# Node chunks of every fourth node, and the loads of a graph-network kernel rearranged over the queues

## The chip, the cores and the metric

The kernel runs on one core of a Trainium2 chip. The metric is the device time of one execution, in microseconds (us). A core has five engines with their own instruction streams: TensorE (PE in the profile) for matmuls, VectorE (DVE), ScalarE (ACT), GpSimd (Pool) and SyncE (SP), which issues DMAs. ACT and Pool issue DMAs too. Engines wait for each other by semaphores; DMA engines, 16 of them, move the data that the queues hand them.

## The reference

Four layers work on x (8 batches, 2048 nodes, 64 channels) with one adjacency matrix adj (2048 × 2048), whose rows hold one value or zero. `_layernorm` is over the channels. Layer 0 has weights of its own for each node:

```python
# layer 0
h = maximum(_layernorm(x), 0)
w = einsum('nd,dkio->nkio', embedding, weight)      # D = 16, K = 3
A_stack = [I, adj, 2 * adj @ adj - I]
x_g = einsum('knm,bmc->bnkc', A_stack, h)
x = x + einsum('bnki,nkio->bno', x_g, w) + embedding @ bias
# layer 1: node 0 set to intervention_value, then three times
effects = einsum('nm,bmd->bnd', adj, v)
v = relu([v, effects] @ W1.T + b1) @ W2.T + b2      # x = x + v
# layer 2: x = x + ((adj @ h) scaled twice, summed, + b_nl) @ w_out.T + b_out
# layer 3: attention, whose mask adj > 0.5 leaves the mean over nodes: x = x + elu(mean(h))
```

## The kernel before

The 8 batches go in four pairs p; a tile of activations holds 128 nodes by (4 node chunks j) by (2 batches × 64 channels), 256 KB, and a pair has four such blocks nb of 512 nodes. Node n of a block is partition n mod 128 of chunk n div 128, so one partition's data of a chunk and batch is a run of 64 floats, 256 B, in x and in the output. The signs of adj stay in SBUF for the whole kernel as `BT` (16 rows m of 128 nodes by 2048), and each product with adj is scaled afterwards by one value per column (`crow`). A product operand is split in a high and a low part (H and L, `halves` L201), so each matmul is done twice. `scaled` (L213, its operation at L214) takes a product out of PSUM times `crow`. DRAM scratch `hs` and `xs` keep the normalised and the running activations; `crowD`, `biasD`, `t1D` and `MD` keep intermediate results.

**The head** (L390 to L468) is what most of the change touches. Rows of adj are loaded (`load_adj` L304) and turned into signs by ACT, two halves each (`signs` L315). The x blocks of pairs 0 and 1 are loaded (`load_x01` L272, `fill_x` at L126), each by two DMAs of 128 KB: one block on ACT's queue, one on SP's, six on Pool's, between the adjacency rows. They are normalised in eight `tick`s (L395), block (0,0), (1,0), (0,1), (1,1) and so on. A norm (`norm_stages` L153) is: mean (L158, L159) and subtraction (L160) on DVE into a tile z, of which there are three buffers (L155); square on ACT (L164); variance on DVE (L167, L168); power −1/2 on Pool (L170); scale on DVE (L173). Then the block is stored to `hs` from SP (L252 to L256), copied to H on ACT (L206) and subtracted to L on DVE (L208). As soon as a row m has its signs and its block is ready, PE does `step` (L415, matmul L418): eight matmuls for pair 0 into four PSUM banks, and, one row later, six for pair 1 into three. These are 224 matmuls of 128 × 128 by 128 × 512.

The order of work is written by hand: `tc.issue_after` puts an instruction behind a named one, `pool_loads` (L307) chains Pool's DMAs behind a given power, and `plan` (L435) says which rows go behind which power. The diagonal blocks of adj (`load_dg`) give the `cols` (`make_cols`), and these the `crow`s (`make_crow`). `bias_loads` (L334) brings the embedding and the bias, `bias_products` (L347 to L361) makes the bias of each node, with the transpose `pe` at L348. The weights `wt` come by six DMAs on SP (L460 to L468), twice the same data for the two halves of the partitions.

**After the head**, the fourth quarter of pair 1's product (L494) is made, t1 is turned back to node order (L499 and before), and for each p and nb there are a second product (L222) and the stage of the node weights (`node_weights` L616): for each of 32 tiles y of a pair, twelve matmuls listed at L632 and eight DVE operations (L641) that add y times one embedding value into `acc` and `odd` by turns. The block is then normalised for the next layer, stored by Pool (`keep` L607 to L613), and a row of `BT` is stored to `MD` (L708). While that runs, SP loads x again (`load_x`), `biasD`, `crow` and others in the order in which the program names them. `layer1` (L763) has three products per pair, `layer2` (L875) one, `finish2` (L835) adds layer 2 and normalises, `outputs` (L859) adds the elu of the mean (L870) and stores (L873), two DMAs per block. For the last pair the queues of these are Pool, SP, ACT and SP for nb 0 to 3.

Of the kernel before, what the change touches and what calls it, by code (L numbers as in the profile page):

```python
# [14 lines left out]
ALU = mybir.AluOpType  # L15
AX = mybir.AxisListType

EPS = 1e-5
# [24 lines left out]
def uniform_path(  # L43
# [65 lines left out]
    make_identity(nc, ident)  # L109
# [3 lines left out]
    order = [nc.gpsimd.memset(mhalf, -0.5)]  # L113

    def part(nb):
        return slice(4 * nb, 4 * nb + 4)

# [5 lines left out]
    def fill_x(acc, layer, p, nb, queue=nc.sync):  # L123
        if layer == 0:
            for bb in range(2):
                ld = queue.dma_start(  # L126
                    acc[:, :, bb * C:(bb + 1) * C],
                    x[2 * p + bb].rearrange("(j p) c -> p j c", p=P)[:, part(nb), :],
                )
            return ld  # L130
        else:
            nc.sync.dma_start(acc, xs[p][:, part(nb), :])
# [13 lines left out]

    pending = []
    powers, firsts, squares, lows, stored = [], [], [], [], []  # L150
    ahead = []

    def norm_stages(xt, name, done, out_):  # L153

        z = block("z", f"z_{name}", 3)  # L155
        g = groups(z)
        mean = small.tile([P, 8], F32, name="mean")
        nc.vector.tensor_reduce(mean, groups(xt), axis=AX.X, op=ALU.add)  # L158
        nc.vector.tensor_scalar(mean, mean, 1.0 / C, None, op0=ALU.mult)  # L159
        firsts.append(nc.vector.tensor_tensor(  # L160
            g, groups(xt), mean[:, :, None].to_broadcast([P, 8, C]), op=ALU.subtract
        ))
        sq = block("sq", f"sq_{name}", 1)
        squares.append(nc.scalar.activation(sq, z, AF.Square))  # L164
        yield
        var = small.tile([P, 8], F32, name="var", bufs=3)
        nc.vector.tensor_reduce(var, groups(sq), axis=AX.X, op=ALU.add)  # L167
        nc.vector.tensor_scalar(var, var, 1.0 / C, EPS, op0=ALU.mult, op1=ALU.add)  # L168
        rstd = small.tile([P, 8], F32, name="rstd", bufs=3)
        powers.append(nc.gpsimd.tensor_tensor(rstd, var, mhalf, op=ALU.pow))  # L170
        yield
        h = z if out_ is None else out_
        nc.vector.scalar_tensor_tensor(  # L173
            groups(h), g, 0.0, rstd[:, :, None].to_broadcast([P, 8, C]), op0=ALU.max, op1=ALU.mult
        )
        done(h)
        yield
# [35 lines left out]
    def scaled(ps, out, crow):  # L213
        ahead.append(nc.vector.tensor_tensor(out, ps, crow, op=ALU.mult))  # L214
        return out
# [36 lines left out]
    def norm_0(p, nb, also=None, xt=None):  # L252

        def done(z):
            stored.append(
                (nc.gpsimd if xt is None else nc.sync).dma_start(hs[p][:, part(nb), :], z)  # L256
            )
            if also is not None:
                also(z)

        norm_relu(load_x(0, p, nb) if xt is None else xt, f"0_{p}_{nb}", done)
# [10 lines left out]
    def load_x01(queue=nc.sync):  # L272
        p, nb = norm_order[len(x01)]
        nm = f"x_{p}_{nb}"
        if p == 1:
            t = term(1, nm).rearrange("p (j f) -> p j f", j=4)
        else:
            t = block("acc" if nb < 2 else "crow", nm, 2)
        loads.append(fill_x(t, 0, p, nb, queue))
        x01.append(t)  # L280
# [23 lines left out]
    def load_adj(m):  # L304
        loads.append(nc.gpsimd.dma_start(BT[:, m, :], adj[m * P:(m + 1) * P, :]))
# [28 lines left out]
    def bias_loads():  # L334
        bd = spare("H", "bd")
        nc.gpsimd.memset(bd, 0.0)
        with tc.issue_after(stored[-1].ins):
            nc.sync.dma_start(emb, embedding.rearrange("(j p) d -> p j d", p=P))
        for j in range(8):
            ld = nc.sync.dma_start(bd[j * D:(j + 1) * D, j * C:(j + 1) * C], bias)  # L340
        bias_tiles.extend((bd, ld))
# [49 lines left out]
    ticks = [0]  # L391
    rests = []
    ticks_at = (0, 1, 2, 3, 4, 6, 8, 10)

    def tick():  # L395
        go_on()
        while rests:
            rests.pop()()
        last = (lows or firsts or [None])[-1]
        k = ticks[0]  # L400
        if k < len(norm_order):
            p, nb = norm_order[k]
            with tc.issue_after(last.ins) if last else nullcontext():
                norm_0(
                    p, nb,
                    lambda z: hls[p].append(
                        halves(z, f"0_{p}_{nb}", prox if p else None, rests)
                    ),
                    x01[k],
                )  # L410
        if lows:
            ahead.append(lows[-1])
        ticks[0] += 1
# [11 lines left out]
    load_x01(nc.scalar)  # L425
    load_x01()

    def lx(_):
        load_x01(nc.gpsimd)

    row, dia = load_adj, load_dg
    pool_loads(order[0], ((row, 0), (lx, 2), (row, 1), (lx, 3), (row, 2)))
    tick()
    tick()
    plan = {  # L435
        0: (0, ((lx, 4),)), 1: (1, ((row, 3), (lx, 5), (row, 4))),
        2: (2, ((lx, 6), (row, 5), (lx, 7))), 3: (3, ((row, 6), (row, 7), (dia, 0), (dia, 1))),
        4: (4, ((row, 8), (row, 9))), 6: (5, ((row, 10), (row, 11), (dia, 2), (dia, 3))),
        8: (6, ((row, 12), (row, 13))), 10: (7, ((row, 14), (row, 15))),
    }  # L440
    for m in range(NCH):
        if m == 12:
            bias_loads()
        if m in ticks_at:
            tick()
        if m in plan:
            pool_loads(powers[plan[m][0]], plan[m][1])
        if m in (11, 13):
            with tc.issue_after(lows[-1].ins):
                for q in (0, 1) if m == 11 else (2, 3):  # L450
                    make_cols(q)

        signs(m, squares[m] if m in (0, 2, 3) else copies[(0, 0, 1, 0, 2, 3, 4, 4, 5, 6, 7)[min(m, 10)]])
        last = step(0, m, banks[0])
        if m > 0:
            with tc.issue_after(last.ins):
                last = step(1, m - 1, banks[1])
        if m in (13, 14):
            with tc.issue_after(last.ins):
                for nb in (0, 1) if m == 13 else (2, 3):  # L460
                    make_crow(nb)
# [3 lines left out]
    for k in range(K):  # L465
        for hf in range(2):
            with tc.issue_after(bias_tiles[1].ins):
                wt_load = nc.sync.dma_start(  # L468
                    wt[hf * C:(hf + 1) * C, k, :].rearrange("i (d o) -> i d o", d=D),
                    weight[:, k].rearrange("d i o -> i d o"),  # L470
                )
    all_done()
# [135 lines left out]
    def keep(p, nb, acc, name, more=None):  # L608

        norm_relu(acc, name, lambda z: nc.gpsimd.dma_start(hs[p][:, part(nb), :], z))  # L610
        if more is not None:
            nc.gpsimd.tensor_tensor(acc, acc, more, op=ALU.add)  # L612
        kept.append(nc.gpsimd.dma_start(xs[p][:, part(nb), :], acc))  # L613
# [3 lines left out]
    def node_weights(p, nb, terms, between=None):  # L617
# [5 lines left out]
        av = acc.rearrange("p j (b c) -> p j b c", b=2)  # L623
        ov = odd.rearrange("p j (b c) -> p j b c", b=2)
# [32 lines left out]
    for p in range(NP):  # L657
# [27 lines left out]
        for nb in range(NB):  # L685
# [20 lines left out]
            with tc.issue_after(kept[-1].ins):  # L706
                m = 4 * p + nb
                nc.gpsimd.dma_start(MD[m * P:(m + 1) * P, :], BTf[:, m, :])  # L708
# [16 lines left out]
    def rows4(r):  # L725
        return r[:, None, :].to_broadcast([P, 4, 2 * C])
# [45 lines left out]
    def layer1(n, p):  # L772
        hl, gT = ops[n]
        steps = 3
        for s in range(steps):
# [3 lines left out]
            def finish(nb):  # L779
                nm = f"1_{p}_{s}_{nb}"  # L780
                if last:
                    acc = load_x(1, p, nb)
                    nc.gpsimd.tensor_tensor(acc, acc, rows4(b2r), op=ALU.add)
                    pn = back_to_nodes(g_new[nb], w2T, nm)
                    nc.vector.tensor_tensor(acc, pn, acc, op=ALU.add)
                    keep(p, nb, acc, f"2_{p}_{nb}", rows4(rbo))
                else:
                    pn = back_to_nodes(g_new[nb], w1e2, nm)
                    nc.vector.tensor_tensor(pn, pn, rows4(r1e), op=ALU.add)
                    hl_new.append(halves(pn, nm))  # L790
# [46 lines left out]
    def finish2(g):  # L837
# [7 lines left out]
        nc.vector.tensor_tensor(acc, pn, acc, op=ALU.add)  # L845
# [14 lines left out]
    def outputs(p):  # L860
# [7 lines left out]
        for nb in range(NB):  # L868
            acc = accs[NB * p + nb]
            (nc.gpsimd if nb == 0 else nc.vector).tensor_tensor(acc, acc, rows4(y), op=ALU.add)  # L870
            queue = (nc.gpsimd, nc.sync, nc.scalar, nc.sync)[nb] if p == NP - 1 else nc.sync
            for bb in range(2):
                queue.dma_start(  # L873
                    out[2 * p + bb].rearrange("(j p) c -> p j c", p=P)[:, part(nb), :],
                    acc[:, :, bb * C:(bb + 1) * C],  # L875
                )
# [635 lines left out]
```

## The time and the profile before

| What | us |
|---|---|
| median of 3 runs | 1280.17 |
| lowest and highest | 1278.7, 1280.47 |
| profiled execution | 1280.51 |
| its span in the profile | 1278.6 |
| outside the span | 1.9 |

| Engine | busy us | share |
|---|---|---|
| PE matmul | 1217.3 | 95% |
| PE weight load | 862.7 | 67% |
| DVE | 751.4 | 59% |
| Pool | 236.8 | 19% |
| ACT | 182.3 | 14% |

A span runs from the first to the last recorded instruction of the core. Busy is the time in which an engine had at least one operation under way; weight loads lie beside matmuls. The granted clock is the share of full speed that PE was allowed. In the DMA views q0 is Pool's queue[...], q1 SP's and q10 ACT's[...]. The time to landing is from the issue of a DMA to the completion that its semaphore tells.

### The profile page before, as it was taken

Reading aid. Unit: us, or ns where it says so; the run is one execution under the profiler, and the core shown is the slowest. Engines: PE = TensorE matmul, PEld = TensorE weight load, DVE = VectorE, ACT = ScalarE, POOL = GpSimd, SP = SyncE. Lnnn points to the kernel's source line nnn. Section 1 sums busy time; section 2 is a strip of 40 time slices with the busy share of each in tenths; the row PEclk is TensorE's granted clock in tenths of the full one; section 3 lists DMA queues with packets and bytes.
Section 4 is the critical chain, followed back from the end, with each engine's and each line's share of the span. In section 5 each row is a group of like instructions: output and inputs, shape, how many; then the busy total and the mean of one; then the engine's idle time right before and its main releaser. Section 6 shows DMA issues by size and latency. Waiting matters only on the chain.

```text
span 1278.6 us, 15515 instructions
## 1 busy us (share of the span) xinstructions
PE 1217.3 (95%) x5702; PEld 862.7 (67%) x5702; DVE 751.4 (59%) x1936; ACT 182.3 (14%) x281; POOL 236.8 (19%) x244
## 2 busy tenths in 40 slices
PE   4899999999999999999999999999999999999993
PEld 3665554555575556755567888787788787788882
DVE  5445887767746776377654446445543554575653
ACT  5530010000010000000011121112111111211100
POOL 6410211111121111011110024004102400432222
PEclk9999999999999999999999999999999999999996
DMA  8982343323332222122255425433643543524321
GB/s 265 343 208 74 96 112 87 90 70 84 95 105 71 71 79 66 65 62 62 67 141 136 102 93 158 112 92 121 150 117 87 159 116 86 161 95 115 108 58 36
DMA packets 140057, 141.14 MB, mean 110 GB/s; under 512 B 95093, under 2 KB 97141, under 8 KB 137925
## 3 DMA queue, kind: packets, MB, share of 16 engines
q1 hardware_dynamic: 121092, 82.05, 25.2%
q0 software_dynamic: 12160, 49.10, 12.8%
q10 hardware_dynamic: 6720, 8.92, 2.5%
q8 instruction: 47, 0.77, 0.2%
q14 instruction: 38, 0.30, 0.1%
HBM read 95.92 MB, written 35.73 MB: 103 GB/s over the span
## 4 chain that ended last, share of the span: by engine, by line
PE 83%; DMA 6%; DVE 4%; issue 3%; POOL 2%; ACT 1%; SPq 0%; ACTq 0%; POOLq 0%; DVEq 0%
PE bv L222 34%; PE y L632 23%; PE bn L587 4%; PE ph L804 3%; PE bv_0b L222 2%; PE bv_2b L222 2%; DMA BT<-in_adj_dram 2%; PE bv_3b L222 2%; PE bv_1b L222 2%; DMA hb<-hs 1%; POOL rstd L170 1%; PE bv_0a L222 1%; PE bv_3a L222 1%; PE bv_2a L222 1%; PE bv_1a L222 1%
## 5 line engine op out<-in xcount | busy, mean ns | idle before, releaser
L222 PE MATMUL bv<-BT,H 128*128 128x512 f32 x1024 | 426.7, 417 | 0.0
L222 PE MATMUL bv<-BT,L 128*128 128x512 f32 x1024 | 401.2, 392 | 0.0
L222 PEld LDWEIGHTS bv<-BT,H 128*128 128x128 f32 x1024 | 192.6, 188 | 47.9 <-issue 11.6
L222 PEld LDWEIGHTS bv<-BT,L 128*128 128x128 f32 x1024 | 192.9, 188 | 47.3 <-issue 11.5
L641 DVE SCALAR_TENSOR_TENSOR acc<-y,emb,acc 128x128 f32<-128x128 f32 x512 | 176.2, 344 | 65.8 <-PE y L632 62.4
L632 PE MATMUL y<-wt,t0T 64*128 64x512 f32 x512 | 144.2, 608 | 10.0 <-DVE odd L641 10.0
L641 DVE SCALAR_TENSOR_TENSOR odd<-y,emb,odd 128x128 f32<-128x128 f32 x448 | 153.3, 342 | 0.0
L170 POOL TENSOR_TENSOR rstd<-var,mhalf 128x8 f32<-128x8 f32 x64 | 107.9, 1688 | 194.5 <-DVE var L168 184.3
L214 DVE TENSOR_TENSOR g<-bv,crow 128x512 f32<-128x512 f32 x48 | 33.2, 691 | 183.7 <-PE bv L222 183.7
L164 ACT ACTIVATE sq<-z 128x512 f32<-128x512 f32 x64 | 40.4, 631 | 406.5 <-DVE z L160 397.4
L632 PEld LDWEIGHTS y<-wt,t0T 64*128 64x128 f32 x512 | 46.7, 187 | 73.9 <-issue 68.0
L612 POOL TENSOR_TENSOR acc<-acc,wl 128x512 f32<-128x512 f32 x16 | 20.6, 1289 | 297.3 <-DVE z L160 297.2
L613 POOL DMA_DIRECT2D xs<-acc x32 | 18.0, 562 | 276.2 <-DVE acc L649 254.2
L632 PE MATMUL y<-wt,t1T 64*128 64x512 f32 x256 | 67.9, 596 | 0.0
L173 DVE SCALAR_TENSOR_TENSOR z<-z,rstd 128x512 f32<-128x512 f32 x64 | 45.9, 723 | 28.2 <-POOL rstd L170 28.2
L587 PEld LDWEIGHTS bn<-wl,g 128*128 128x128 f32 x384 | 49.5, 191 | 6.3 <-ACT H L206 1.6
L167 DVE TENSOR_REDUCE var<-sq 128x8 f32<-128x512 f32 x64 | 43.5, 679 | 15.8 <-ACT sq L164 15.8
L587 PE MATMUL bn<-wl,g 128*128 128x128 f32 x384 | 51.1, 276 | 1.0 <-DVE var L168 0.5
L749 DVE SCALAR_TENSOR_TENSOR junk<-mt,cols,st 128x512 uint8<-128x512 bf16 x64 | 50.8, 794 | 0.6
L632 PEld LDWEIGHTS y<-wt,t1T 64*128 64x128 f32 x256 | 27.7, 188 | 27.3 <-issue 27.3
L809 ACT ACTIVATE g<-g,b1s 128x512 f32<-128x512 f32 x32 | 23.2, 724 | 139.4 <-DVE g L808 139.3
L160 DVE TENSOR_TENSOR z<-acc,mean 128x512 f32<-128x512 f32 x56 | 38.3, 690 | 6.6 <-DMA hs<-z 5.2
(209 smaller groups left out, 1677.3 us busy)
## 6 DMA issues: line engine op xcount, KB each, us to landing
BT<-in_adj_dram POOLq DMA_DIRECT2D x16, 1024.0 KB, 9.2
crow<-crowD SPq DMA_DIRECT2D x64, 256.0 KB, 3.2
st<-in_adj_dram SPq DMA_DIRECT2D x64, 256.0 KB, 3.4
hs<-z POOLq DMA_DIRECT2D x40, 256.0 KB, 2.8
xs<-acc POOLq DMA_DIRECT2D x32, 256.0 KB, 2.5
MD<-BT POOLq DMA_DIRECT2D x16, 512.0 KB, 5.0
acc<-xs SPq DMA_DIRECT2D x32, 256.0 KB, 3.2
hb<-hs SPq DMA_DIRECT2D x28, 256.0 KB, 3.6
```

The costliest lines, as they stand in the source:

```text
L160: firsts.append(nc.vector.tensor_tensor(g, groups(xt), mean[:, :, None].to_broadcast([P, 8, C]), op=ALU.subtract))
L164: squares.append(nc.scalar.activation(sq, z, AF.Square))
L167: nc.vector.tensor_reduce(var, groups(sq), axis=AX.X, op=ALU.add)
L170: powers.append(nc.gpsimd.tensor_tensor(rstd, var, mhalf, op=ALU.pow))
L173: nc.vector.scalar_tensor_tensor(groups(h), g, 0.0, rstd[:, :, None].to_broadcast([P, 8, C]), op0=ALU.max, op1=ALU.mult)
L214: ahead.append(nc.vector.tensor_tensor(out, ps, crow, op=ALU.mult))
L222: nc.tensor.matmul(ps, hl[m // 4][i][:, m % 4, :], BT[:, m, nb * 512:(nb + 1) * 512], start=(m == 0 and i == 0), stop=(m == NCH - 1 and i ...
L587: nc.tensor.matmul(ps[:, t, :], fT[:, t * P:(t + 1) * P], wmat, start=True, stop=True)
L632: nc.tensor.matmul(y[:, bb, :], terms[k][hs_, ts], wt[hs_, k, dg * 512:(dg + 1) * 512], start=(k == 0), stop=(k == K - 1),)
L641: last = nc.vector.scalar_tensor_tensor(xj, yd, ec, old, op0=ALU.mult, op1=ALU.add)
L749: nc.vector.scalar_tensor_tensor(junk, mt, cols[:, i, :], st, op0=ALU.mult, op1=ALU.not_equal, accum_out=bad[:, i, q:q + 1],)
L804: fill[12] = lambda: nc.tensor.matmul(ph, w1v2 if s else w1vT, gT[nb], start=True, stop=True)
```

## The change

Node n of a block is now partition n div 4, chunk n mod 4: four consecutive nodes lie in one partition. So x, the embedding and the output move in runs of four nodes (1 KB for x and the output, 256 B for the embedding), and a row m of `BT` and `MD` holds every fourth node of a block. Inside a tile that is read from x the order is batch, chunk, channel; helpers give the view that an operation needs (`nodes`, `split`, `each`). `scaled` writes its columns permuted, so that what follows finds the chunks together.

The loads of x go on SP, all eight at its start, one DMA for each block; Pool loads adj alone, seven rows at once, then rows behind the powers of a new plan. The ident tile is made without its helper, its two operations ahead of the loads. The ticks are replaced by `norm_block`, which puts a whole norm on DVE in one order, every second row. Three weight loads are followed by three copies within SBUF. The last pair's stores are one DMA per block, blocks 1, 2, 0, 3 in order, blocks 0 and 2 from ACT, 1 and 3 from SP.

```diff
+    def rows_of(a, m):
+        return a.rearrange("(b p t) n -> b t p n", p=P, t=4)[m // 4, m % 4]
+    def runs_of(a, p, nb):
+        return a[2 * p:2 * p + 2].rearrange("e (b p t) c -> b p e (t c)", p=P, t=4)[nb]
+    def runs(acc):
+        return acc.rearrange("p j f -> p (j f)").rearrange("p (e r) -> p e r", e=2)
+    def nodes(acc):
+        return acc.rearrange("p j f -> p (j f)").rearrange("p (e j c) -> p j e c", e=2, c=C)
...
         if layer == 0:
-            for bb in range(2):
-                ld = queue.dma_start(
-                    acc[:, :, bb * C:(bb + 1) * C],
-                    x[2 * p + bb].rearrange("(j p) c -> p j c", p=P)[:, part(nb), :],
-                )
+            return queue.dma_start(runs(acc), runs_of(x, p, nb))
...
     def scaled(ps, out, crow):
-        ahead.append(nc.vector.tensor_tensor(out, ps, crow, op=ALU.mult))
+        ps, crow = (a.rearrange("p (q t) -> p q t", t=4) for a in (ps, crow))
+        to = out.rearrange("p (t q) -> p q t", t=4)
+        ahead.append(nc.vector.tensor_tensor(to, ps, crow, op=ALU.mult))
...
+    def norm_block(k):
+        stage(k, 0)
+        low()
+        stage(k, 1)
+        stage(k, 2)
...
-    load_x01(nc.scalar)
-    load_x01()
-    pool_loads(order[0], ((row, 0), (lx, 2), (row, 1), (lx, 3), (row, 2)))
-    tick()
-    tick()
+    for _ in norm_order:
+        load_x01(nc.sync)
+    pool_loads(order[0], tuple((row, m) for m in range(7)))
+    for i in range(3):
+        stage(0, i)
+        if i == 2:
+            low()
+        stage(1, i)
     plan = {
...
+        1: (1, ((row, 7), (row, 8))), 2: (2, ((row, 9), (row, 10))),
+        3: (3, ((row, 11), (dia, 0), (dia, 1))), 4: (4, ((row, 12),)),
+        5: (5, ((row, 13), (dia, 2), (dia, 3))), 6: (6, ((row, 14), (row, 15))),
     }
...
     for k in range(K):
-        for hf in range(2):
...
+            wt_load = nc.sync.dma_start(
+                wt[:C, k, :].rearrange("i (d o) -> i d o", d=D),
+                weight[:, k].rearrange("d i o -> i d o"),
+            )
+    with tc.issue_after(wt_load.ins):
+        for k in range(K):
+            nc.sync.dma_start(wt[C:, k, :], wt[:C, k, :])
...
         odd = l0q.tile([P, 4, 2 * C], F32, name="odd")
-        av = acc.rearrange("p j (b c) -> p j b c", b=2)
-        ov = odd.rearrange("p j (b c) -> p j b c", b=2)
+        av, ov = nodes(acc), nodes(odd)
...
-        for nb in range(NB):
+        for nb in (1, 2, 0, 3):
...
-            (nc.gpsimd if nb == 0 else nc.vector).tensor_tensor(acc, acc, rows4(y), op=ALU.add)
-            queue = (nc.gpsimd, nc.sync, nc.scalar, nc.sync)[nb] if p == NP - 1 else nc.sync
-            for bb in range(2):
-                queue.dma_start(
-                    out[2 * p + bb].rearrange("(j p) c -> p j c", p=P)[:, part(nb), :],
-                    acc[:, :, bb * C:(bb + 1) * C],
-                )
+            (nc.gpsimd if nb == 0 else nc.vector).tensor_tensor(
+                nodes(acc), nodes(acc), rows4(y), op=ALU.add
+            )
+            queue = nc.scalar if nb % 2 == 0 and p == NP - 1 else nc.sync
+            queue.dma_start(runs_of(out, p, nb), runs(acc))
```

The signs of each row stand behind a named norm operation on ACT: rows 2 and 3 behind the square of the third block, rows 4 and 5 behind that of the fourth, and so on; the `crow`s are made two rows later, at rows 14 and 15. The embedding is loaded by the same grouping in one DMA of 256 B runs, still behind the last norm's store to `hs`.

## The prediction

> **What bounds the kernel now.** I read the table of windows first, then the waits of TensorE (PE), then the chain of what ended last. Over the span PE is busy 95%, so only its gaps can be shortened, and the windows show most of them at the start. The columns are the busy time and count of each engine, the granted clock, the DMA share and GB/s.
>
> ```profile
> 0.00:20.00 20.00, 4.88 (x12) 3.83 (x13) 10.36 (x23) 9.68 (x12) 12.49 (x22) 1.00 0.87 263
> 20.00:40.00 20.00, 16.45 (x62) 11.95 (x61) 11.01 (x23) 9.87 (x13) 15.07 (x16) 0.92 0.95 289
> 40.00:60.00 20.00, 18.41 (x75) 13.57 (x74) 9.70 (x30) 13.74 (x17) 8.71 (x11) 0.99 0.94 337
> 60.00:80.00 20.00, 19.05 (x90) 14.69 (x89) 6.39 (x23) 8.91 (x9) 1.97 (x4) 1.00 1.11 280
> ```
>
> PE's busy time hides how little is done; its counts tell. The chain steps back-to-back matmuls by 0.23 us, so 20 us hold about 88: the first two windows hold 12 and 62. Meanwhile the DMA engines are 87 to 95% busy. PE's waits, in us in all, times and longest:
>
> ```profile
> PE bv_0a L418 <- ACT H L206: 15.1, 1, 15.1
> PE y L632 <- DVE odd L641: 10.0, 7, 2.9
> ...
> PE bv_0a L418 <- ACT BT L319: 4.5, 4, 1.9
> ```
>
> The first is the start: nothing to multiply until 15.1 us. The second lies in the y stage. The last of the head's chain, and the stall behind the second (start, duration):
>
> ```profile
> 33.48 10.97 DMA BT<-in_adj_dram
> ...
> 54.14 9.42 DMA BT<-in_adj_dram
> 63.58 2.01 ACT BT L319 x2
> ```
> ```profile
> 411.13 4.61 DMA crow_3b<-crowD
> ```
>
> So the head is bound by the arrival of adjacency rows (L305), which come when Pool issues them, and from 65.6 us by PE. Its steps end with the transpose `pe` at 81.5.
>
> [...]While adjacency rows (8 KB packets, q0) stream beside embedding packets of 64 B on SP's queue (q1), the DMA view of 64 to 68 us has one for one; in 70 to 71 us, when q0 runs dry, q1 leaps:
>
> ```profile
> q0 software_dynamic: 225, 1.61, 102.6%
> q1 hardware_dynamic: 226, 0.01, 32.5%
> ```
> ```profile
> q1 hardware_dynamic: 1189, 0.08, 92.2%
> q0 software_dynamic: 32, 0.13, 34.9%
> ```
>
> A small packet thus costs its queue the whole of an 8 KB packet in between. [...]No row of before writes fp32 with a 512 B stride.
>
> **The head, step by step.** Removed from Pool: six x blocks, 12 issues, in pairs of about 1.5 us (9 us); adj rows 0 to 6 are then issued back to back at 0.57 us. Added on SP: eight x DMAs of 256 KB at its start. The first normalised block also needs no Pool issue between its two powers and its data: I put PE's first matmul at 10.5 instead of 15.1.
>
> But SP's queue also carries the stores hs<-z (L256). In before it has one x block ahead of them; in after all eight. DVE's fourth subtract, z of block (1,1), reuses the first of three z buffers (L155), and waits until that buffer's hs store has landed. Behind it on DVE stand L of block (0,1) and every later norm; behind its square on ACT stand the signs of row 4; so PE can do rows 0 to 3 (32 matmuls of pair 0, 18 of pair 1: 50), to about 24 us, and then waits. When does the store land?
> - x has 8 × 256 = 2048 packets of 1 KB. Adj data starts at 4.2 us in before; here the ident operations (0.20 and 0.30 us on Pool's timeline) move ahead of the first issue: 4.5. From about 2.4 to 4.5 at 284 GB/s (a window of before) some 600 to 640 pass; 1408 are left, 88 for each of 16 engines.
> - One for one they go with 88 adj packets per engine, rows 0 to 10, all issued by then. A pair took 4 us × 16 / 225 = 0.284 us with 64 B; 1 KB at 20 GB/s per engine (16 share about 330) adds 0.05: 0.33. So x ends at 4.5 + 88 × 0.33 = 33.5. Where the other packet is dearer (0.38), 37.9.
> - The store follows. Such stores landed in 7.9 us (median) beside adj, 2.5 at the best: I take 4, so 37.5 to 38; both ends 36 and 46.
>
> From 38: subtract 0.69, square 0.63, half a sign 1.04, so row 4 at 40.4. Left are 224 − 50 = 174 matmuls × 0.2276 (20 us / 88) = 39.6, four groups of pt_c 1.9, and 2 for the clock: at 15.1 to 19.6 in before matmuls start 0.43 apart. That is 83.9 against 81.5, **+2.4**. ACT, DVE and Pool need about 5.7 us for each block of two rows after the stall (L170 alone 1.7 to 2.0), PE 28 × 0.2276 = 6.4, so PE bounds. Rows 11 to 15 are issued behind later powers, the last at about 58, landing in some 6; PE wants row 15 after 78. Pool's waits of rows 8 to 15 for a DMA semaphore of an older row can delay the powers queued behind, but those rows landed long before. Moved later, crow and t1T steps (two t1T evictions of 0.69 us ahead of crow copies): **+0.5**, ends 0 and 2.
>
> **Other parts.**
> - Weights: six loads become three and three on-chip copies which wait on SP for them. Six issues took 7.3 us, to 79.7 in before; loads landed in 6.6. wt is used at 91 (DVE) and 104 (PE). Here the embedding and the bias loads, which stand behind the last norm's store, go out at about 66 (55.3 before); the embedding's landing (16.7 before, a quarter of the packets now) falls before `pe` at 82 or a little past it, the weights follow near 74, and two landings end by 88: 0 for all, up to +2 if the copies crawl. Behind them on SP stand only small loads and crow_0b, wanted when bv_0b ends at 104.
> - x in one DMA instead of two, everywhere: SP issues less ahead of crow. In the chain of the stall at 411 us SP spends 0.38 and 1.20 us on the two x issues (L126) just before crow_3b; one goes: −1. For the six other waits of y on DVE, whose parts I did not trace, −0.5: **−1.5**, from −5 (half of the 10.0) to +1.
> - `scaled` (L214, 96 evictions of 0.69 us) writes with stride 512 B. Doubled, 66 us of DVE time, most of it hidden: DVE is 59% busy, and only L587 <- e (2.5 us) and a few stage starts wait on it. **+0.5**, from 0 to +3.
> - Pool adds L612/L783 (1.3 us) and L870 over four dimensions: **+0.3**, from 0 to 1; they are off the chain.
> - L641 writes two runs of 64 instead of 128 elements, same count: 0.
> - The last stores. In before:
>
> ```profile
> 1263.16 1.76 POOL L870 TENSOR_TENSOR acc<-acc,y 128x512 f32<-128x512 f32 x1 [4.19 <-DVE y L867]
> 1263.84 3.51 SPq L873 DMA_DIRECT2D out_dram<-acc  x4
> 1265.22 1.57 POOL L873 DMA_DIRECT2D out_dram<-acc  x2 [0.29 <-POOL acc L870]
> ```
>
>  Pool's two issues are the last piece of the chain. On ACT, which has nothing else to do then (0.96 for two), and one DMA per block: **−1**, from −2 to 0. DVE's last add, not Pool, then comes last.
>
> Sum 2.4 + 0.5 − 1.5 + 0.5 + 0.3 − 1 = **+1.2**. Against the profiled execution's 1280.5 (span 1278.6, 1.9 outside) this is 1281.7; the median of the runs is 0.3 lower: 1281.4. About 0.2%, 2.6 us, is what a measurement can tell from no change; so the likeliest case is "no change".
>
> **The rivals.**
> - *x drains early* (faster). If the engines pass more than about two x packets per adj packet, the store lands before PE runs out of rows 0 to 3 (about 22 us) and the early start is kept: 10.5 + 224 × 0.2276 + 1.9 + 2.4 + some 3 of arrival gaps = 69, −12.5; with the rest, −13.7: 1266. For it: engines and packets are of another size here. Against it: 226 to 225.
> - *The store lands late* (slower). Same place, dearer pairs (0.38) and a landing of 7.9: 37.9 + 7.9 = 45.8, each us after 38 one us at the end, +7.8: 1289. It decides above about 39.5, where the sum passes +2.6. For it: hs<-z took a median of 7.9 in this head. Against it: no adj rows are left beside it if both streams end together.
> - *The y stage becomes bound by DVE* (slower). Eight L641 follow every y tile at 0.26 us each, 2.1 of 2.6 us; DVE idles 0.36 to 0.51 us per tile. If the two-run form costs over 0.05 us more, it is bound; at 0.10 each, 128 tiles × 0.35 = +45: 1325.[...]
>
> **How the numbers follow.** The likeliest case, 0.62, own range 1276 to 1287 (store landing 36 to 42, the other bounds partly cancelling): of it 0.12 faster, 0.26 same, 0.24 slower. Early drain 0.20, faster. Late landing 0.13 and y stage 0.05, slower. Together 0.32 faster, 0.26 same, 0.42 slower. The range, 1265 to 1289, reaches to the middle of both head rivals, leaving out about 0.1 at each side.
>
> **What would show it.** In the head of after: SP's hs<-z landing from 14 to 38 us after issue; DVE's fourth z idle before on DMA hs; ACT's sign of row 4 near 39; PE's first matmul near 10.5, a PE gap from 24 to 40, then 88 per 20 us and `pe` near 84. At equal share q0 and q1 should have equal packet counts in 5 to 30 us. L214 near 0.69 us, L641 near 0.34, no Pool issue at the end. I am wrong if the fourth z starts before 25, if rows, not z, are what PE waits for after 40, or if the y windows change.

## The result, and the profile after

The changed kernel takes 1284.47 us (median of 4 runs, 1281.74 to 1285.98) against 1279.43 us of the kernel before in the same comparison (1277.09 to 1280.47): a ratio of 1.004, with a 95% interval of 1.0016 to 1.0063. It is slower by about 5 us. The forecast was 1281.4 with a range of 1265 to 1289; its most likely single side was slower (0.42), though its most likely case was "no change". The profiled execution took 1285.3, with a span of 1283.5 (before 1278.6).

The windows of the head, in the columns of the prediction (PE, weight loads, DVE, ACT, Pool, clock, DMA share, GB/s):

```profile
0.00:20.00 20.00, 7.28 (x26) 5.89 (x27) 10.63 (x22) 11.12 (x14) 11.65 (x21) 1.00 0.94 336
20.00:40.00 20.00, 5.71 (x26) 4.39 (x24) 0.54 (x2) 1.41 (x2) 0.14 (x1) 0.73 1.01 383
40.00:60.00 20.00, 17.18 (x66) 13.52 (x67) 12.99 (x25) 15.12 (x19) 10.04 (x11) 0.84 0.67 203
60.00:80.00 20.00, 20.00 (x90) 16.49 (x89) 9.70 (x41) 13.72 (x16) 4.64 (x5) 1.00 0.89 242
```

The second row is the whole story of the head: in 20 us PE starts 26 matmuls (62 before), DVE two operations and Pool one, while the DMA engines never rest. PE, DVE and Pool all wait, in the end, for one transfer. What PE waits for, in us in all, times, longest:

```profile
PE bv_0a L460 <- ACT BT L348: 16.8, 1, 16.8
PE bv_0a L460 <- ACT H L230: 12.7, 1, 12.7
PE y L681 <- DVE odd L690: 7.9, 7, 2.3
PE bn L637 <- DVE e L241: 4.4, 2, 4.1
```

The start is earlier (12.7 against 15.1), but a stall of 16.8 us follows that the kernel before does not have. The wait named is a sign on ACT; the chain of what ended last says what that sign stood behind (start, duration):

```profile
10.17 29.79 DMA hs<-z
40.07 0.70 DVE z L181
```

The first block's store to `hs` was issued at 10.17 and landed 29.8 us later; only then could DVE overwrite that z buffer. The DMA view of 20 to 25 us shows why it took so long: Pool's rows of adj (q0) and SP's x blocks (q1) pass one for one (packets, MB, share of 16 engines).

```profile
q1 hardware_dynamic: 248, 0.24, 17.5%
q0 software_dynamic: 247, 1.81, 89.8%
```

Outside the head one row of the groups changed clearly, the eviction of the products (mean ns after the busy time). Its row in the kernel before stands first:

```profile
L214 DVE TENSOR_TENSOR g<-bv,crow 128x512 f32<-128x512 f32 x48 | 33.2, 691 | 183.7 <-PE bv L222 183.7
```
```profile
L241 DVE TENSOR_TENSOR g<-bv,crow 128x512 f32<-128x512 f32 x48 | 51.8, 1080 | 176.2 <-PE bv L249 176.2
L690 DVE SCALAR_TENSOR_TENSOR acc<-y,emb,acc 128x128 f32<-128x128 f32 x512 | 176.1, 344 | 62.0 <-PE y L681 61.9
L662 POOL TENSOR_TENSOR acc<-acc,wl 128x512 f32<-128x512 f32 x16 | 20.6, 1287 | 299.7 <-DVE z L181 299.6
```

The other two, which also got new layouts, are where they were (344 and 1289 ns before).

To see where 4.9 us of span come from, I read the start of the same instruction in both traces at five borders and took the lengths between them:

| Stretch | before us | after us | difference |
|---|---|---|---|
| start to the end of the head's steps | 81.5 | 86.5 | +5.0 |
| from there to the first bv_0b | 13.1 | 14.5 | +1.4 |
| the rest of layer 0 | 557.5 | 554.4 | −3.1 |
| layer 1, first product to last ph | 449.8 | 453.5 | +3.7 |
| layer 2, to the last pS | 157.8 | 161.9 | +4.0 |
| from the last pS to the end of the span | 18.8 | 12.8 | −6.0 |

The head's steps are taken to end where the first matmul of pair 1's fourth quarter (L494, L544 after) starts. So a change that moves the total by 0.4% moves single stretches by up to 6 us, in both directions. Each column is one profile, and profiles of the same code differ too: e3 below, whose code is that of before up to the last stores, has 79.9, 13.1, 555.9, 449.8 and 160.4 in the first five rows. So the rows are good to about 2.5 us, and only layer 1 is much better: 449.4 to 449.9 in the four versions with the eviction of 691 ns, 453.5 to 454.6 in the six that differ from these by an eviction of 1071 to 1080 ns. Layer 1's part can be watched at one border of its steps. First the kernel before, then the kernel after (start, duration, and in brackets PE's idle time):

```profile
687.70 0.69 DVE L214 TENSOR_TENSOR g<-bv,crow 128x512 f32<-128x512 f32 x1 [1.98 <-PE bv L222]
688.43 0.69 DVE L808 TENSOR_TENSOR g<-ph,g 128x512 f32<-128x512 f32 x1
689.15 0.72 ACT L809 ACTIVATE g<-g,b1c 128x512 f32<-128x512 f32 x1 [4.16 <-DVE g L808]
690.01 1.08 PE L587 MATMUL bn<-wl,g 128*128 128x128 f32 x8
```
```profile
690.93 1.09 DVE L241 TENSOR_TENSOR g<-bv,crow 128x512 f32<-128x512 f32 x1 [1.99 <-PE bv L249]
692.06 0.69 DVE L857 TENSOR_TENSOR g<-ph,g 128x512 f32<-128x512 f32 x1
692.78 0.72 ACT L858 ACTIVATE g<-g,b1c 128x512 f32<-128x512 f32 x1 [4.56 <-DVE g L857]
693.56 1.16 PE L637 MATMUL bn<-wl,g 128*128 128x128 f32 x8 [0.17 <-ACT g L858]
```

The product's eviction, an addition, a relu and PE's bn follow each other with hardly any slack; PE comes to bn at 2.31 us after the eviction's start before and 2.63 after. From step to step through the twelve steps of layer 1 the same matmul lies 3.2, then 3.6, 4.0, 4.2, 4.6, 5.0, 5.1, 5.5, 5.9, 6.1, 6.5 and 6.9 us later than before: about 0.4 at eight of the eleven borders, 0.1 to 0.3 at the other three.

### The profile page after: what moved, and what is told of

The parts are those of the page before. It is cut to its first block, busy times and chain, and to the rows that moved or that the text cites. A ratio compares the mean times of both kernels' runs of the same rounds, so it can differ in the third digit from the quotient of the medians.

```text
span 1283.5 us, 15389 instructions
## 1 busy us (share of the span) xinstructions
PE 1216.8 (95%) x5702; PEld 863.5 (67%) x5702; DVE 782.7 (61%) x1936; ACT 182.0 (14%) x281; POOL 224.5 (17%) x230
## 4 chain that ended last, share of the span: by engine, by line
PE 84%; DVE 6%; DMA 5%; ACT 1%; POOL 1%; issue 1%; POOLq 0%; ACTq 0%; SPq 0%; DVEq 0%
PE bv L249 33%; PE y L681 24%; PE bn L637 4%; PE ph L853 3%; PE bv_1b L249 2%; DMA hs<-z 2%; PE bv_2b L249 2%; PE bv_0b L249 2%; PE bv_3b L249 2%; PE bv_0a L249 1%; PE bv_3a L249 1%; PE bv_2a L249 1%; PE bv_1a L249 1%; PE pS L902 1%; PE pt L261 1%
## 5 line engine op out<-in xcount | busy, mean ns | idle before, releaser
L249 PEld LDWEIGHTS bv<-BT,H 128*128 128x128 f32 x1024 | 193.1, 189 | 47.9 <-issue 11.6
L241 DVE TENSOR_TENSOR g<-bv,crow 128x512 f32<-128x512 f32 x48 | 51.8, 1080 | 176.2 <-PE bv L249 176.2
L662 POOL TENSOR_TENSOR acc<-acc,wl 128x512 f32<-128x512 f32 x16 | 20.6, 1287 | 299.7 <-DVE z L181 299.6
L798 DVE SCALAR_TENSOR_TENSOR junk<-mt,cols,st 128x512 uint8<-128x512 bf16 x64 | 48.0, 750 | 0.5
```

The lines of the kernel that those rows point to most:

```text
L241: ahead.append(nc.vector.tensor_tensor(to, ps, crow, op=ALU.mult))
L249: nc.tensor.matmul(ps, hl[m // 4][i][:, m % 4, :], BT[:, m, nb * 512:(nb + 1) * 512], start=(m == 0 and i == 0), stop=(m == NCH - 1 and i ...
L798: nc.vector.scalar_tensor_tensor(junk, mt, cols[:, i, :], st, op0=ALU.mult, op1=ALU.not_equal, accum_out=bad[:, i, q:q + 1],)
```

## The experiments

Ratios are to the kernel before on the same chip, with 95% intervals; medians of it were 1279.1 to 1280.3.

**The store's queue (e2_hs_act).** From the changed kernel:

```diff
-                (nc.gpsimd if xt is None else nc.sync).dma_start(hs[p][:, part(nb), :], z)
+                (nc.gpsimd if xt is None else nc.scalar).dma_start(hs[p][:, part(nb), :], z)
```

> The changed kernel with the eight hs stores of the head issued by ACT instead of SP[...]. Theory A[...]: the first store lands 4 to 9 us after its issue instead of 29.8, DVE's fourth subtraction starts near 20.5 instead of 40.07, PE's gap of 16.8 us shrinks to a few us of waits for x (x still shares one for one with adj, its last block landing near 33 to 38), the head's steps end 12 to 17 us earlier, near 70 to 74; in all 1268 to 1273. Rival B (the DMA engines are simply full until about 38 us, whatever the queue): the store still lands after 25 us or more, and the time moves by less than 4 us, 1280 to 1285. Rival C (x itself is what comes late next): the fourth subtraction is early but blocks 5 to 8 wait for x, and the head's steps end only 5 us earlier, near 1279.

1268.55 us, ratio 0.9898 (0.9872 to 0.9924). This one word is worth 16 us against the changed kernel and makes the version 1% faster than the kernel before. The stores' landing (least, median, most) and the second window of this version:

```profile
DMA to landing us min/median/max: 7.3/7.7/8.7
```
```profile
20.00:40.00 20.00, 19.83 (x86) 15.57 (x84) 12.67 (x26) 14.31 (x18) 9.72 (x11) 1.00 1.07 409
```

The DMA engines are no less full than in the changed kernel (409 against 383 GB/s), so rival B falls: what delayed the store was not the load on the engines but the x blocks ahead of it in its own queue. Three queues now share, in 20 to 25 us x and adj still with equal counts, with the stores on ACT's queue (q10) between them:

```profile
q0 software_dynamic: 231, 1.64, 81.3%
q1 hardware_dynamic: 229, 0.22, 16.0%
q10 hardware_dynamic: 117, 0.21, 10.9%
```

PE does 86 matmuls in a stretch where it did 26; the steps end at 70.6 (86.5). Rival C falls too: after the start DVE waits for x once, 0.27 us, at the eighth block.

**The dense eviction (e1_dense).** From the changed kernel:

```diff
-        ps, crow = (a.rearrange("p (q t) -> p q t", t=4) for a in (ps, crow))
-        to = out.rearrange("p (t q) -> p q t", t=4)
-        ahead.append(nc.vector.tensor_tensor(to, ps, crow, op=ALU.mult))
+        ahead.append(nc.vector.tensor_tensor(out, ps, crow, op=ALU.mult))
```

> The changed kernel with scaled writing its columns in the order in which it reads them; the permutation of the nodes is left out, so what follows meets the nodes of a block in another order; all instructions and their number stay. Theory A (the strided write itself costs 0.39 us on each of 96 evictions, and where PE waits for one it is on the path): the eviction falls from 1080 to about 690 ns, the drift in layer 1 (+3.7 us from 655 to 1079 us) and the wait bn<-e of 4.1 us in layer 2 (with the slower clock after it +4.0) go, and about 1 us of the way from the end of the head's steps to bv_0b; in all 8 to 9 us less than the changed kernel, near 1276, 3 to 4 us faster than the kernel before. Theory B (the evictions are hidden, and the later layers drift for another reason, the new layouts of acc or the Pool additions): L241 falls but the time stays within 2 us of the changed kernel, 1282 to 1285.

This version and e10 leave the permutation out and so compute something else than the reference; they only price the eviction.

1276.22 us, ratio 0.9967 (0.9951 to 0.9982), 8.2 below the changed kernel, and 8.1 below e4, which was measured beside it on the same chip: theory A. The eviction is back at 692 ns, and layer 1 takes 449.9 us (449.8 before, 453.5 after), so its drift is the eviction's. From the head's steps to bv_0b it takes 0.7 us less than the changed kernel, about as expected. One part of the expectation failed: the wait bn<-e in layer 2 stayed, at 3.6 us.

**The stride on the other side (e4_swap).** From the changed kernel:

```diff
-        ps, crow = (a.rearrange("p (q t) -> p q t", t=4) for a in (ps, crow))
-        to = out.rearrange("p (t q) -> p q t", t=4)
+        ps, crow = (a.rearrange("p (q t) -> p t q", t=4) for a in (ps, crow))
+        to = out.rearrange("p (t q) -> p t q", t=4)
```

> The changed kernel with the two loops of scaled exchanged: it writes densely and reads the product and crow with a stride of 16 B; what is computed is the same. Theory A1 (only the write's stride costs[...]): 690 ns, and the time is that of the dense version, 8 to 9 us less than the changed kernel, near 1276. Theory A2 (a stride costs on whichever side it lies): 1050 to 1400 ns, time as the changed kernel, 1284, or up to 6 us more.

1284.33 us, ratio 1.0028 (1.0017 to 1.0038):

```profile
L241 DVE TENSOR_TENSOR g<-bv,crow 128x512 f32<-128x512 f32 x48 | 51.4, 1071 | 176.7 <-PE bv L249 176.6
```

Theory A2: a read with a stride of 16 B costs VectorE what a write with 512 B costs, 1071 against 1080 ns. Reordering the loops does not help.

**Both at once (e10_dense_hs).** The edits of e1 and e2 together.

> Both single edits at once: hs stores of the head on ACT, and scaled dense with the permutation of the nodes left out (what follows meets the nodes of a block in another order). Theory A (the two losses are independent and add): 1268.5 - 8.2 = 1260.3, within 2. Rival (they share time, the evictions of the head's end being hidden once PE starts early): 1263 to 1266.

1262.61 us, ratio 0.9858 (0.9828 to 0.9888), at the border between the two: the dense eviction is worth 5.9 us here, not 8.2, by medians (7.3 by the spans of the profiles, 1260.3 and 1267.6). The losses are mostly independent; whether the rest is overlap or the spread of few runs stays open.

**The permutation in the weight loads (e5_best).** From e2: dense `scaled`, and

```diff
+    def chunk(t, i):
+        return t.rearrange("p (q t) -> p t q", t=4)[:, i, :]
...
-        pt = transposed(lambda t: src[:, t * P:(t + 1) * P], f"t1_{p}_{nb}")
+        pt = transposed(lambda t: chunk(src, t), f"t1_{p}_{nb}")
...
-            nc.tensor.matmul(ps[:, t, :], fT[:, t * P:(t + 1) * P], wmat, start=True, stop=True)
+            nc.tensor.matmul(ps[:, t, :], chunk(fT, t), wmat, start=True, stop=True)
...
-                            y[:, bb, :], terms[k][hs_, ts], wt[hs_, k, dg * 512:(dg + 1) * 512],
+                            y[:, bb, :], chunk(terms[k][hs_], t), wt[hs_, k, dg * 512:(dg + 1) * 512],
```

> The changed kernel with the head's hs stores on ACT, and the permutation moved from VectorE to where it may be hidden: scaled writes and reads densely, and the matmuls that take a feature-major tile as their weights (y, bn, pt_t) load every fourth column (stride 16 B); ScalarE's copy of the transposed h writes with that stride. What is computed is the same. Theory A ([...]weight loads lie beside other matmuls and can bear a stride): 1268.5 - 8 = about 1260. Rival D (a strided weight load is dearer than a dense one, as the evictions were, and y's loads of 187 ns are no longer hidden behind matmuls of some 215 ns): at half as much again, 94 ns on some 2000 loads, up to 190 us more, 1300 to 1450.

1344.4 us, ratio 1.0503 (1.0471 to 1.0535). Rival D, at less than its upper end. The weight loads of bn and y:

```profile
L640 PEld LDWEIGHTS bn<-wl,g 128*128 128x128 f32 x384 | 93.3, 325 | 3.0 <-ACT g L860 1.5
L683 PEld LDWEIGHTS y<-wt,t0T 64*128 64x128 f32 x512 | 78.2, 311 | 51.6 <-issue 41.2 <-PE y L683 4.5
```

They took 191 and 187 ns before. Where the matmuls between are short, as at bn, the load is no longer hidden: a group of eight bn takes 1.90 us in most places (1.08 before), and layer 1, with most of the bn, 507.5 us (449.8). ScalarE's copies, which now write with the stride, also rose, from 587 to about 1090 ns, but PE waited for them 4.4 us in all.

**The permutation in the streamed operand (e8_moving).** From e2: dense `scaled`, crow copied once in the order wanted, and

```diff
+    def wide(m, nb):
+        return BT[:, m, nb * 512:(nb + 1) * 512].rearrange("p (q t) -> p t q", t=4)
...
-                    ps, hl[m // 4][i][:, m % 4, :], BT[:, m, nb * 512:(nb + 1) * 512],
+                    ps, hl[m // 4][i][:, m % 4, :], wide(m, nb),
```

> The changed kernel with the head's hs stores on ACT, and the permutation moved into TensorE's reading: each product with adj streams its 512 columns of BT with a stride of 16 B (every fourth column, four times over), so that it comes out in the order that is wanted, and scaled is dense; the four crows of the head are copied in that order once. What is computed is the same. Theory A (matmuls of 128 x 512 stay at 0.227 us each[...]): evictions of 690 ns and the head of the version with hs on ACT, 1268.5 - 8 = about 1260. Rival D (a stride costs PE as it costs the weight loads, 187 to 306 ns in the version before, and VectorE, 691 to 1080 ns): each of some 3300 product matmuls takes 0.1 to 0.2 us more, 1600 to 1900 us in all.

1954.38 us, ratio 1.5262 (1.5218 to 1.5306). Rival D, somewhat above its range. The row of before stands first:

```profile
L222 PE MATMUL bv<-BT,H 128*128 128x512 f32 x1024 | 426.7, 417 | 0.0
```
```profile
L252 PE MATMUL bv<-BT,H 128*128 128x512 f32 x1024 | 695.8, 679 | 0.0
```

Of the four places tried for the permutation, VectorE's eviction is the cheapest.

**The last store's queue (e3_tail).** From the kernel before:

```diff
-            queue = (nc.gpsimd, nc.sync, nc.scalar, nc.sync)[nb] if p == NP - 1 else nc.sync
+            queue = (nc.scalar, nc.sync, nc.scalar, nc.sync)[nb] if p == NP - 1 else nc.sync
```

> The kernel before with one edit: the last pair's first block is stored from ACT, not from Pool; still two DMAs of 256 B runs each. Theory A (a transfer of Pool's at the end of the program holds its end up): the time from the last issue to the end of the span falls from 11.8 to about 5.5 us, and the time by 5 to 6 us, to 1274. Rival B (the 6 us between the two tails come from fewer and larger runs): the time falls by 0 to 1.5 us, as the chain's last Pool piece goes. My forecast had -1 for it.

1276.07 us, ratio 0.9961 (0.9948 to 0.9974): −4.2 us, between the two. From the last pS to the end of the span it takes 15.7 us instead of 18.8, so 3.1 of the 6 us of the tail; the others, if one profile of each can be trusted so far, come from the rest of the edit.

**Pool's store put back, and two DMAs per block (e6_pool_tail, e9_two_stores).** From the changed kernel, one each:

```diff
-            queue = nc.scalar if nb % 2 == 0 and p == NP - 1 else nc.sync
+            queue = (nc.gpsimd, nc.sync, nc.scalar, nc.sync)[nb] if p == NP - 1 else nc.sync
```
```diff
-            queue.dma_start(runs_of(out, p, nb), runs(acc))
+            if p < NP - 1:
+                queue.dma_start(runs_of(out, p, nb), runs(acc))
+            else:
+                for e in range(2):
+                    queue.dma_start(runs_of(out, p, nb)[:, e, :], runs(acc)[:, e, :])
```

> The changed kernel with one edit: the last pair's first block is stored by Pool again, now one DMA of 1 KB runs. Theory A (a Pool transfer at the end holds the end up by about 3 us, as the tail of the kernel before showed when it was taken away: 18.8 to 15.7 us from the last pS to the end of the span; the other 3 us of the two tails come from one DMA of 1 KB runs in place of two of 256 B): the tail grows from 12.8 to about 15.5 to 16 us, the time to 1287. Rival (all 6 us go back to Pool here): the tail is near 18.8 us, the time 1290.

> The changed kernel with one edit: the last pair's output blocks are stored by two DMAs each again (1 KB runs, ACT and SP as before). From the last pS to the end of the span it takes 12.8 us in the changed kernel, 15.7 in the kernel before with Pool's store taken away, 18.8 in the kernel before. Theory A (the number of DMAs at the end counts): the tail is near 15.5 us. Rival (their 256 B runs count): it stays within 0.7 us of 12.8.

1284.81 us, ratio 1.0043 (1.003 to 1.0056), with a tail of 13.3 us; and 1283.82, ratio 1.0035 (1.0022 to 1.0048), with a tail of 12.5. Both answers of e6's expectation are wrong, and my theory of Pool with them; e9 goes to its rival. Tails of the other versions with the changed kernel's stores lie between 11.6 and 13.4, so with 1 KB runs neither Pool's queue nor the number of DMAs costs anything that shows. What is left of the edit, besides the order of the blocks and all that changed earlier, are the runs of 256 B. That is by elimination; no run has 256 B runs in the new layout, and the traces speak against a simple price of runs. The busy tenths of the DMA engines from 1262 to 1290 us (40 slices of 0.7 us), in before, e3 and after:

```profile
DMA  0002865969870000000000000000000000000000
DMA  0029999988100000000000000000000000000000
DMA  0000000000000000000567599200000000000000
```

Read in slices of 0.1 us, the last packets of the stores pass 10.8, 10.8 and 9.9 us after the last pS. The rest of the tail, 8.0, 4.9 and 2.9 us, lies behind them (3.4 in e6, 2.5 in e9). So about 1 us of the 6 lies in the transfers and 5 behind the last packet, where the profile shows next to nothing. Nor do counts of packets lead on: in before a block of 256 KB in runs of 256 B is 96 packets on Pool's queue and 1056 on ACT's.

**Two loads of x per block (e7_x_two).** From the changed kernel, behind the head:

```diff
-        fill_x(acc, layer, p, nb, queue)
+        if layer == 0:
+            for e in range(2):
+                queue.dma_start(runs(acc)[:, e, :], runs_of(x, p, nb)[:, e, :])
+        else:
+            fill_x(acc, layer, p, nb, queue)
```

> The changed kernel with one edit: behind the head, each load of x for layer 0 is two DMAs of 128 KB (1 KB runs) again instead of one. Theory A (the 3.1 us that layer 0 behind the head gained, from 557.5 to 554.4 us, come from fewer issues on SP ahead of crow): layer 0 is back near 557, the time 1286 to 1287. Rival (they come from the larger runs, or are no more than one profile differs from the next): layer 0 stays within 1 us of 554.4, the time 1284 to 1285.

1282.86 us, ratio 1.0023 (1.0009 to 1.0038), and layer 0 behind the head takes 552.1 us, no more than the changed kernel's 554.4 (1.6 us of that difference lie in its first product, at a granted clock of 1.00 in e7 and 0.83 in after). Theory A falls: the gain of layer 0 does not come from fewer issues on SP. The larger runs, which e7 keeps, stay possible.

## Why the prediction came out as it did

The side with the largest chance and the range held; the likeliest case did not: it was a sum of +1.2 in which three terms were too small, two of them losses and one a gain. That the total came within 4 us is in good part luck: the two terms of the head were short by 3.5 us and `scaled` by 7 to 8, the tail by 5 the other way.

**The head: the mechanism was right, the size short.** The prediction had the store land at 37.5 to 38, PE's stall from 24 to 40 and `pe` at 84. Measured: 39.96, a stall from 25.7 to 42.5, and the end of the steps at 86.5 (`pe` itself at 87.1, after a wait for a crow copy). So the first term, said to be +2.4, was +5.0; the second, +0.5, was +1.4, of which e1's dense evictions take back 0.7. The step that was short is the time of x. Its pair price was right: from 5 to 35 us 1452 packets of x pass beside 1452 of adj, 0.33 us a pair on each engine. Its start was not: by 4.5 us 550 packets of SP's queue had passed, not 600 to 640 (284 GB/s for 2.1 us are some 580), and the last x block landed at about 36, not 33.5. The store landed 4 us behind it, as was said. From the stall on the sum was right: 174 matmuls and the four transposes took 44.0 us against 43.5. The rival in which x drains early is refuted by the equal counts (they show equal shares, not whether single packets alternate or groups of them); the late landing was said to decide above 39.5, and the store is just beyond it. That the store would follow the x blocks ahead of it on SP's queue was an assumption of mine; e2, where the eight stores land in 7.3 to 8.7 us, against 29.8 for the first one in after, shows that this order, not the load, is the cause. The first matmul was said for 10.5 and came at 12.7, since ACT first worked through the two sign halves of row 0 (10.16 to 12.16) before H; it cost nothing, as PE stalled later anyway.

**`scaled` failed in its size.** It was set at +0.5 with a bound of +3; e1 measures 8.2, of the 37 us that 96 evictions of 0.39 more make. The term had two halves. The price: +0.39 us per eviction was inside what was bounded (a doubling). The exposure was not: I took the evictions to be hidden because DVE is 59% busy and only bn<-e and a few stage starts waited for them. A wait of almost zero is not slack: at each border of layer 1 the eviction was already part of a chain that reached PE just in time, so the 0.4 showed in full at most borders (+3.7, all of which e1 takes back). By the spans of the profiles e1 gains 7.7 us; besides these 3.7 there are 1.7 in layer 2, 0.4 up to the first bv_0b and 1.9 in layer 0 behind it. Of these last, 1.6 are not the eviction's: they lie in the first product, at a clock of 1.00 in e1 and 0.83 in after, and e4 and e7, with evictions as dear as in after, have them too. So where the eviction's cost lies outside layer 1 is only partly known. The waits that it was listed under were a poor guide: the longest bn<-e in layer 2 is 1.3 us in the kernel before, 4.1 after, 3.6 in e1 and 1.2 in e10, whose evictions are all dense; e3, with the code of before up to there, has 2.3. A lower clock goes with it: in the first fifth of that stretch it is 1.00 in before and e10, 0.95 in e1 and e3, 0.89 in after. So part of layer 2's +4.0 is how profiles differ, and the cause of that is open.

The doubling was an estimate of mine, with no trace behind it. Measured, the write with a stride of 512 B takes 1080 ns against 691, and the read with one of 16 B 1071 (e4). There the product and `crow` are both read with the stride, and they were not tried apart.

**The tail was a gain of 6, said to be 1.** The price was read from the chain, whose last piece is Pool's issue. But the chain ends with the last instruction that the profile records: in before, the last store's issue ends 11.2 us before the end of the span, in after 5.5, and I took that rest for fixed. It is not:

```profile
1275.91 2.05 ACTq L923 DMA_DIRECT2D out_dram<-acc  x2
```

e3 shows that taking the first block's store from Pool's queue shortens it in the kernel before (−4.2 us by medians), e6 that giving it back costs nothing that shows in the kernel after. For the other 3 us e6 and e9 leave the short runs, or some other part of the edit. What fills the time after the last packet, 8.0 us in the kernel before and 2.9 after, no view shows.

**The middle had the right sign by a wrong cause.** −1.5 was said for fewer issues on SP; layer 0 gains 3.1, and e7 shows that issues are not why. The stall at 411 us is where most of it lies: in after, e1, e6 and e7 the stretch from 402 to 435 us is 2.8 to 3.0 us shorter than in the profile of before; but e3, whose code there is that of before, is also 1.7 shorter, so part of it is how one profile differs from the next. In after the store xs<-acc goes out ahead of z instead of behind it, so that x is loaded earlier, and crow_3b lands sooner (3.3 us in e7, 4.6 in before). Whether the earlier store, the larger runs of x ahead of crow_3b on SP's queue, or both count was not separated.

**What held:** L641 (344 and 344 ns), the Pool additions (1289 and 1287), and the weights, which no wait of PE names; and after 42.5 us PE waited for the signs of rows only 0.3 us in all. The rival of a y stage bound by DVE is refuted by L641; that its two-run form costs no more was an assumption until then.

## What to carry to other kernels

Before a bulk load is put at the front of a queue, ask which small transfers will stand behind it there and who reuses their buffers: here eight stores on another queue, of which the first was the one waited for, decided 16 us. Where a step sits on a chain with no wait, price each tenth of a microsecond in full for every time it is passed, whatever the engine's busy share. And read the time between the last recorded instruction and the end of the span; it can change. Before a difference of 2 us in one stretch is explained, read that stretch in another profile whose code there is the same.

## What the runs showed of the hardware beyond the expected

- Two queues with work shared the DMA engines by number of packets, not by bytes: 248 of 1 KB beside 247 of up to 8 KB, so SP's queue had 0.24 of 2.05 MB in those 5 us.
- A stride of 16 B in the operands cost time: on VectorE 1071 against 691 ns for 128 × 512 fp32, as much as a write with 512 B (1080); on TensorE a weight load of 64 × 128 311 against 187 ns, and a matmul that streams 512 such columns 679 against 417 ns.
- On ScalarE a copy of 128 × 512 that wrote with a stride of 16 B took about 1090 ns against 587 (e5).
- Four output blocks at the end of the program: in runs of 256 B the end of the span came 15.7 us after the last pS, or 18.8 with one block on Pool's queue; in runs of 1 KB 11.6 to 13.4, whatever the queue and the number of DMAs. Most of the difference lies after the last packet (8.0, 4.9 and 2.9 us in before, e3 and after), and its cause is open.
